# Attention's output in two array steps instead of three, with GELUs on pieces of the pairs

## The chip, the cores and the metric

The kernel runs on one core of a Trainium2 chip. The metric is the device time of one execution in microseconds (us), the median of repeated runs. The core has TensorE (matmul products), VectorE (DVE), ScalarE (ACT), GpSimd (POOL) and SyncE (SP), which issues most of the transfers. The engines work side by side, each through its own list of instructions, and wait for one another at semaphores.

## The reference, cut to what matters

Two layers on a picture of 384 channels and 192 x 192 points. The change concerns the first layer, whose attention runs over channels: 8 heads of 48 channels, 9,216 points after pooling.

```python
x = x + L0(gn(x), ...)                         # gn: group norm, 32 groups
x = x + L1(gn(x), ...)                         # signs, shifted by channel, times signs of weights

def L0(x, ...):                                # cut
    qkv = einsum('bchw,oc->bohw', x, w_qkv) + b_qkv
    qkv = qkv.reshape(b, 3*c, 96, 2, 96, 2).max(axis=(3, 5))
    qkv = conv_3x3_depthwise(qkv, w_dw) + b_dw
    q, k, v = split(qkv, 3)                    # each (8 heads, 48, 9216)
    q, k = q / norm(q), k / norm(k)
    attn = einsum('bhcn,bhdn->bhcd', q, k) * temperature
    out = sum(topk_softmax(attn, n) @ v * a    # four sizes n of top-k
              for n, a in ...)
    out = gelu(out, approximate=False)
    out = repeat(repeat(out, 2, axis=2), 2, axis=3)
    return einsum('bchw,oc->bohw', out, w_proj) + b_proj
```

The four softmaxes are one 48 x 48 matrix per head in the end, and "attention's output" is that matrix times v, per head, followed by the GELU.

## The kernel before

The picture is cut into 24 units of 8 rows. A first pass takes the group norm's sums, a second makes q and k and their products, a third makes v. In the third pass each unit has three steps, one for each group of 128 channels of v. One step is:

```python
def qkv_unit(pqkv, xt, u, m, pl, parts, before=None):
    for r0, nr, c0, ncol in BLOCKS:                       # three blocks of 512 points
        ps = pqkv.tile([P, 512], F32, name="qkv")         # 3 PSUM buffers
        for t in range(CT):
            nc.tensor.matmul(ps, wq[:, t, m*P:(m+1)*P], x4[:, t, ...], ...)       # L351
        nc.vector.tensor_reduce(pl[...], ps..., AX.XY, ALU.max)                   # L358, pooling
    ...
    nc.scalar.activation(new, new, AF.Identity, bias=bq[:, m:m+1])                # L367, the bias
    for acc, r0, n in parts:                              # one chunk, or two at a chunk's edge
        for k in range(9):                                # the 3 x 3 taps
            if k == 0:
                nc.scalar.activation(acc2, src, AF.Identity, bias=..., scale=...) # L374, first tap
            else:
                nc.vector.scalar_tensor_tensor(acc2, src, wdw[...], acc2, ...)    # L376
    if u < NU - 1:
        nc.scalar.copy(pl[:, 0:2, :], pl[:, PR:PR+2, :])                          # L378, the halo
```

v comes to lie in `chunk`, four units to a chunk. Heads go in pairs of 96 channels (`PAIR`), of which there are four (`NP`). Pair p has partitions 32p to 32p+31 (`Q` = 32) of all three groups t: in group 0 the first 32 channels of its first head, in group 1 the first 32 of its second head, and in group 2 the last 16 of both. `aT` holds the matrices, laid out to match, with zeros between the two heads. Whenever a block of 512 points (there are `NAB` = 18) is complete, its output is computed, and written over v:

```python
def attention(g):
    c, b = divmod(g, CPX // ABLK)
    cols = slice(b * ABLK, (b + 1) * ABLK)
    pss = [po.tile([P, ABLK], F32, name="ops") for _ in range(NP)]    # 4 PSUM banks in all
    for t in range(CT):
        for p in range(NP):
            rows = slice(p * Q, (p + 1) * Q)
            nc.tensor.matmul(                                          # L625
                pss[p][:PAIR],
                aT[rows, t, p * PAIR : (p + 1) * PAIR],
                chunk[c][rows, t, cols],
                start=(t == 0), stop=(t == CT - 1),
            )
    for p, ps in enumerate(pss):
        for t in [p] if p < CT else range(CT):
            src, to = (slice(0, PAIR),) * 2 if p < CT else (slice(t * Q, (t + 1) * Q), slice(PAIR, P))
            nc.scalar.activation(chunk[c][to, t, cols], ps[src], AF.Gelu,
                                 accum_out=osum[to, t, g : g + 1])     # L635

for u in range(NU):
    ...
    for m in range(CT):
        qkv_unit(pqkv, xt, u, 2 * CT + m, pool[m], parts)
        ...                                        # softmaxes in pieces, until steps == ()
        elif steps == () and done < NAB - HOLD and (done + 1) * ABLK <= first * WP:
            attention(done)
            done += 1
```

The last two blocks (`HOLD` = 2) come in the tail, where the order is set by hand. Elsewhere a scheduler sets the order of each engine's instructions when the program is built; it keeps the waits, but not the order of the text. After the tail comes the last stage: projection, signs, and the second layer's products.

Of the kernel before, what the change touches and what calls it, by code (L numbers as in the profile page):

```python
# [15 lines left out]
AF = mybir.ActivationFunctionType  # L16
# [4 lines left out]
P = 128  # L21
C = 384
CT = C // P
# [4 lines left out]
HD = C // HEADS  # L28
# [14 lines left out]
HALF = P // 2  # L43
# [8 lines left out]
ABLK = 512  # L52
NAB = NPX // ABLK
# [23 lines left out]
PAIR = 2 * HD  # L77
NP = C // PAIR
Q = P // NP
HOLD = 2  # L80
# [67 lines left out]
def conv_preact_kernel(ctx: ExitStack, tc: tile.TileContext, a: dict, out: bass.AP):  # L148
    nc = tc.nc
# [27 lines left out]
    def unit(u, pool=big, parts=1, pieces=1):  # L177
        xt = pool.tile([P, CT, UPX], F32, name="xt", tag="big")
        n = CT // parts
        for t in range(0, CT, n):  # L180

            for j in range(0, UPX, UPX // pieces if t == CT - 1 else UPX):
                px = slice(j, j + UPX // pieces if t == CT - 1 else UPX)
                nc.sync.dma_start(xt[:, t : t + n, px], xv[u][:, t : t + n, px])  # L184
        return xt
# [15 lines left out]
    def group_sums(ps, s):  # L201

        for t in range(CT):
            nc.tensor.matmul(ps, ind[:, t, :], s[:, t], start=(t == 0), stop=(t == CT - 1))
# [8 lines left out]
    def right(name, bufs=1, stack=att):  # L213
        return stack.enter_context(tc.tile_pool(name=name, bufs=bufs, side="right"))
# [4 lines left out]
    osum = ap.tile([P, CT, NAB], F32, name="osum")  # L219
    aT = right("aT").tile([P, CT, C], F32, name="aT")  # L220
# [35 lines left out]
    with tc.tile_pool(name="p1", bufs=1, side="right") as p1, tc.tile_pool(name="p1ps", bufs=2, space=PSUM) as psp:  # L256
# [17 lines left out]
        for i in range(NU):  # L274
# [8 lines left out]
            for t in range(CT):  # L283
                if t == (u + 1) % SHARE:
                    at = NB + i // SHARE
# [8 lines left out]
                b, k = divmod(seen[t], BATCH)  # L294
                seen[t] += 1
                for j in range(UPX // 512):
                    at = (k * (UPX // 512) + j) * 6
# [5 lines left out]
        with tc.manual_schedule():  # L303
# [5 lines left out]
            ps = psp.tile([NG, 2], F32, name="gsps")  # L309
# [13 lines left out]
            ps = [psp.tile([P, 1, 2], F32, name=f"spread{t}", bufs=1) for t in range(CT)]  # L323
# [15 lines left out]
    def rows(u):  # L339

        return (1 if u else 2), (PR if u < NU - 1 else PR + 1)
# [41 lines left out]
    with pairs, tc.tile_pool(name="p2t", bufs=2, side="right") as tp:  # L383
# [59 lines left out]
        for u in range(NU):  # L443
# [6 lines left out]
            n = hi - lo + 1  # L450
# [11 lines left out]
    def gathered():  # L462

        products(NU - 1)
        for t in range(CT):
            at = D0[t] - B0[t] * B
            nc.vector.tensor_copy(gsb[:, t, : DN[t]], gram[t][:, at : at + DN[t]])
        last_products.close()
# [104 lines left out]
    def opened(name, bufs, **kw):  # L573
        return end.enter_context(tc.tile_pool(name=name, bufs=bufs, reuse_waits="tile", **kw))
# [25 lines left out]
    chunk = []  # L600
    with ExitStack() as vs:
        wp = vs.enter_context(tc.tile_pool(name="p4w", bufs=1, side="right", reuse_waits="tile"))
        scratch = vs.enter_context(ExitStack())
        p3 = right("p3", stack=scratch)
        vs.enter_context(products_of_x)

        pool = first_pooled
        for t in pool:
            nc.gpsimd.memset(t[:, 0:2, :], 0.0)  # L609
        done, steps = 0, None  # L610

        def weights(name):
            wl = wp.tile([P, CT, C], F32, name="wl")
            tc.keep_in_program_order(nc.scalar.dma_start(wl, a[name].rearrange("(t p) o -> p t o", p=P)))
            return wl

        def attention(g):

            c, b = divmod(g, CPX // ABLK)
            cols = slice(b * ABLK, (b + 1) * ABLK)  # L620
            pss = [po.tile([P, ABLK], F32, name="ops") for _ in range(NP)]
            for t in range(CT):
                for p in range(NP):
                    rows = slice(p * Q, (p + 1) * Q)
                    nc.tensor.matmul(  # L625
                        pss[p][:PAIR],
                        aT[rows, t, p * PAIR : (p + 1) * PAIR],
                        chunk[c][rows, t, cols],
                        start=(t == 0),
                        stop=(t == CT - 1),  # L630
                    )
            for p, ps in enumerate(pss):
                for t in [p] if p < CT else range(CT):
                    src, to = (slice(0, PAIR),) * 2 if p < CT else (slice(t * Q, (t + 1) * Q), slice(PAIR, P))
                    nc.scalar.activation(chunk[c][to, t, cols], ps[src], AF.Gelu, accum_out=osum[to, t, g : g + 1])  # L635

        for u in range(NU):
            xt = kept.pop(NU + u) if NU + u in kept else unit(u)
            if u == NU - 1:
                for i, f in enumerate(FIRST):  # L640
                    kept[f] = unit(f, big if i else early)
            if u % UC == 0:
                chunk.append(big.tile([P, CT, CPX], F32, name="chunk", tag="big"))
            lo, hi = rows(u)
            first = PR * u - 2 + lo
            last = first + hi - lo
            for m in range(CT):
                parts = []
                for c in range(first // CR, last // CR + 1):
                    r0, r1 = max(first, c * CR), min(last, c * CR + CR - 1)  # L650
                    parts.append(
                        (chunk[c][:, m, (r0 - c * CR) * WP : (r1 + 1 - c * CR) * WP], r0 - first, r1 + 1 - r0)
                    )
                qkv_unit(pqkv, xt, u, 2 * CT + m, pool[m], parts)
                if m == 0 and u == UC:

                    wl = weights("w_projG").rearrange("p t (g c) -> p t g c", c=GRP)
                    tc.keep_in_program_order(nc.vector.tensor_reduce(wg1, wl, AX.X, ALU.add))
                if m == 0 and u == 1:
                    tc.keep_in_program_order(  # L660
                        nc.scalar.dma_start(wpr, a["w_projT"].rearrange("(t p) o -> p t o", p=P))
                    )
                if m == 0 and u == UC + 1:
                    tc.keep_in_program_order(nc.scalar.activation(wb, weights("weightT"), AF.Sign, saturate=False))
                if u == 0 and m == CT - 1:
                    gathered()
                    po = vs.enter_context(tc.tile_pool(name="p4o", bufs=NP, space=PSUM))
                    psp = vs.enter_context(tc.tile_pool(name="p3ps", bufs=1, space=PSUM))
                    bg = psp.tile([P, P], F32, name="p3ps")[:NG, :1]
                    group_sums(bg, bpr.unsqueeze(2))  # L670
                    nc.vector.tensor_scalar_mul(bg1, bg, -1.0 / GRP)
                if u >= TOPK and steps is None:
                    steps = softmaxes(p3, psp)
                if steps:
                    if next(steps, 1):
                        steps = ()
                        scratch.close()
                        early = opened("p5x0", 1)
                elif steps == () and done < NAB - HOLD and (done + 1) * ABLK <= first * WP:
                    attention(done)  # L680
                    done += 1
        kept[FIRST[1] - 1] = unit(FIRST[1] - 1)
        with tc.manual_schedule():

            assert done == NAB - HOLD
            for g in range(done, NAB - 1):
                attention(g)
            for m in range(CT):
                projected(pqkv.tile([P, 512], F32, name="qkv")[:, :PPX], FIRST[0], m)
            attention(NAB - 1)  # L690

            projected(pqkv.tile([P, 512], F32, name="qkv")[:, :PPX], FIRST[1], 0)
            nc.vector.tensor_reduce(om, osum, AX.X, ALU.add)
            ys = [pqkv.tile([P, 512], F32, name="qkv")[:, :PPX] for m in range(1, CT)]
            projection(ys[0], FIRST[1], 1)
            projection(ys[1], FIRST[1], 2, range(1))
            ps = psp.tile([P, P], F32, name="p3ps")[:NG, :1]
            for t in range(CT):
                nc.tensor.matmul(ps, wg1[:, t], om[:, t : t + 1], start=(t == 0), stop=(t == CT - 1))
            nc.vector.tensor_scalar(gm, ps, -1.0 / (GRP * NPX), bg1, ALU.mult, ALU.add)  # L700
            projection(ys[1], FIRST[1], 2, range(1, 2))
            ps = psp.tile([P, P], F32, name="p3ps")[:, :CT].unsqueeze(2)
            spread(ps, gm)
            projection(ys[1], FIRST[1], 2, range(2, CT))
            added(ys[0], FIRST[1], 1, 0)
            nc.vector.tensor_add(nmean1, nmean0, ps[:, :, 0])
            added(ys[0], FIRST[1], 1, 1)
            for r in range(2):
                added(ys[1], FIRST[1], 2, r)
# [203 lines left out]
```

## Time and profile before

| | before |
|---|---|
| median of 3 runs | 2239.83 us (2238.95 to 2241.53) |
| span of the profiled execution | 2237.0 us |
| TensorE busy | 2085.8 us, 93% |
| VectorE busy | 1902.5 us, 85% |
| ScalarE busy | 819.6 us, 37% |
| GpSimd busy | 210.8 us, 9% |
| granted TensorE clock | 1.0 |
| products of attention's output (L625) | 432 records, 52.0 us busy |
| their GELUs (L635) | 108, of 587 ns each |

Each fp32 matmul of the text is two records in the profile, a pair of passes. A line of groups reads: source line, engine, operation, what is written <- what is read, shape, count, then busy time, mean duration in ns, and the idle time of the engine before these instructions with what ended it. A line of a timeline reads: start in us, duration in us, engine, source line, operation, tensors, shape, count, and in brackets the idle time before it and what ended that. A line of windows gives the stretch, its length, and per engine the busy time and the number of instructions.

### The profile page before, as it was taken

Reading aid. Unit: us, or ns where it says so; the run is one execution under the profiler, and the core shown is the slowest. Engines: PE = TensorE matmul, PEld = TensorE weight load, DVE = VectorE, ACT = ScalarE, POOL = GpSimd, SP = SyncE. Lnnn points to the kernel's source line nnn. Section 1 sums busy time; section 2 is a strip of 40 time slices with the busy share of each in tenths; the row PEclk is TensorE's granted clock in tenths of the full one; section 3 lists DMA queues with packets and bytes.
Section 4 is the critical chain, followed back from the end, with each engine's and each line's share of the span. In section 5 each row is a group of like instructions: output and inputs, shape, how many; then the busy total and the mean of one; then the engine's idle time right before and its main releaser. Section 6 shows DMA issues by size and latency. Waiting matters only on the chain.

```text
span 2237.0 us, 19501 instructions
## 1 busy us (share of the span) xinstructions
PE 2085.8 (93%) x6135; PEld 989.3 (44%) x6135; DVE 1902.5 (85%) x3267; ACT 819.6 (37%) x1419; POOL 210.8 (9%) x329
## 2 busy tenths in 40 slices
PE   0049999999999999999999999999999999999998
PEld 0024444444444444444444444443444444455555
DVE  5668888888888888888888898987787878899998
ACT  4542222222222222222222221225333232398876
POOL 1000000000000000000000000000000000077765
PEclk9999999999999999999999999999999999999999
DMA  9962222222222222222222312105221212379997
GB/s 398 418 274 64 64 68 70 75 95 70 69 64 68 70 74 95 70 69 64 68 70 72 98 30 105 53 11 211 85 85 43 87 67 101 127 277 407 424 425 328
DMA packets 209719, 302.66 MB, mean 135 GB/s; under 512 B 162224, under 2 KB 165072, under 8 KB 209616
## 3 DMA queue, kind: packets, MB, share of 16 engines
q1 hardware_dynamic: 199296, 248.18, 31.8%
q10 hardware_dynamic: 10320, 53.25, 5.8%
q8 instruction: 48, 0.79, 0.1%
q14 instruction: 55, 0.45, 0.1%
HBM read 216.04 MB, written 56.62 MB: 122 GB/s over the span
## 4 chain that ended last, share of the span: by engine, by line
PE 81%; DVE 10%; DMA 5%; ACT 1%; SPq 1%; issue 0%; DVEq 0%; ACTq 0%
PE qkv L351 64%; PE l1ps L792 6%; PE yps L580 6%; DVE chunk L376 5%; DMA xt<-in_x_dram 5%; PE gram L433 3%; DVE pooled L358 2%; PE ops L625 2%; DVE dw L376 1%; SPq L184 1%; DVE xt L592 1%; ACT chunk L374 0%; PE qkv L270 0%; ACT pooled L367 0%; SPq L422 0%
## 5 line engine op out<-in xcount | busy, mean ns | idle before, releaser
L351 PE MATMUL qkv<-xt,wq 128*128 128x512 f32 x3888 | 1679.2, 593 | 0.0
L351 PEld LDWEIGHTS qkv<-xt,wq 128*128 128x128 f32 x3888 | 735.1, 190 | 918.1 <-issue 821.9
L376 DVE SCALAR_TENSOR_TENSOR dw<-pooled,small,dw 128x384 f32<-128x384 f32 (+2 forms) x1152 | 708.7, 615 | 118.8 <-ACT dw L374 93.7
L358 DVE TENSOR_REDUCE pooled<-qkv 128x128 f32<-128x512 f32 x648 | 442.5, 684 | 67.1 <-PE qkv L351 66.8
L376 DVE SCALAR_TENSOR_TENSOR chunk<-pooled,small,chunk 128x384 f32<-128x384 f32 (+3 forms) x696 | 369.5, 545 | 70.9 <-ACT chunk L374 53.7
L378 ACT COPY pooled<-pooled 128x196 f32<-128x196 f32 x207 | 73.6, 356 | 761.5 <-DVE dw L376 542.8
L367 ACT ACTIVATE pooled<-pooled,small 128x384 f32<-128x384 f32 x216 | 133.0, 616 | 402.8 <-DVE pooled L358 389.4
L773 ACT ACTIVATE signs<-xt,nmean 64x1536 fp8e4<-64x1536 f32 x144 | 226.5, 1573 | 41.7 <-PE yps L580 26.0
L792 PE MATMUL l1ps<-signs,wb 128*128 128x384 fp8e4 x864 | 152.2, 326 | 0.0
L580 PE MATMUL yps<-chunk,wpr 128*128 128x384 f32 x396 | 138.2, 487 | 2.7 <-DVE xt L592 2.7
L270 PE MATMUL qkv<-wq,late 128*32 128x384 f32 x18 | 9.0, 665 | 140.3 <-ACT late L292 140.3
L801 DVE SCALAR_TENSOR_TENSOR xt<-l1ps,small,xt 128x768 f32<-128x768 f32 x144 | 138.3, 1007 | 0.0
L592 DVE SCALAR_TENSOR_TENSOR xt<-yps,small,xt 128x768 f32<-128x768 f32 x132 | 128.1, 1012 | 10.8 <-PE yps L580 4.4
L298 DVE BATCH_NORM_STATS2 room<-xt 128x6 f32<-128x512 f32 x144 | 88.1, 678 | 51.0 <-DMA xt<-in_x_dram 50.9
L609 POOL MEMSET pooled<- 128x196 f32 x3 | 0.8, 263 | 1300.6 <-DVE dw L376 1300.6
L456 ACT ACTIVATE sq<-dw 128x384 bf16<-128x384 f32 (+2 forms) x144 | 75.3, 523 | 112.4 <-DVE dw L376 112.4
L792 PEld LDWEIGHTS <-wb 128*128 128x128 fp8e4 x864 | 83.7, 97 | 72.3 <-issue 14.2
L374 ACT ACTIVATE dw<-pooled,small 128x384 f32<-128x384 f32 (+2 forms) x144 | 100.4, 697 | 2.2
L287 ACT ACTIVATE room<-xt 128x1536 bf16<-128x1536 f32 x48 | 71.2, 1483 | 66.4 <-DMA xt<-in_x_dram 65.7
L580 PEld LDWEIGHTS yps<-chunk,wpr 128*128 128x128 f32 x396 | 73.2, 190 | 44.3 <-issue 3.6
L404 DVE STREAM_TRANSPOSE blocks<-dw 128x384 f32<-128x384 f32 (+1 forms) x144 | 82.0, 569 | 3.4
L751 POOL COPY rest<-signs 9x384 int32<-9x384 int32 (+1 forms) x144 | 72.4, 503 | 64.5 <-ACT signs L773 59.0
(115 smaller groups left out, 622.1 us busy)
## 6 DMA issues: line engine op xcount, KB each, us to landing
xt<-in_x_dram SPq DMA_DIRECT2D x81, 2304.0 KB, 13.4
out_dram<-xt ACTq DMA_DIRECT2D x17, 2304.0 KB, 15.6
room<-blocks SPq DMA_DIRECT2D x736, 36.0 KB, 2.0
xt<-in_x_dram SPq DMA_DIRECT2D x26, 768.0 KB, 9.0
out_dram<-xt ACTq DMA_DIRECT2D x12, 768.0 KB, 8.7
out_dram<-xt SPq DMA_DIRECT2D x8, 768.0 KB, 3.4
wq<-in_w_qkvT_dram ACTq DMA_DIRECT2D x1, 1728.0 KB, 15.1
room<-blocks SPq DMA_DIRECT2D x32, 48.0 KB, 2.0
```

What stands on the lines that cost most here:

```text
L298: nc.vector.bn_stats(stats[b][:, t, at : at + 6], xt[:, t, j * 512 : (j + 1) * 512])
L351: nc.tensor.matmul(ps, wq[:, t, m * P : (m + 1) * P], x4[:, t, r0 : r0 + nr, c0 : c0 + ncol], start=(t == 0), stop=(t == CT - 1),)
L358: nc.vector.tensor_reduce(pl[:, 2 + r0 // 2 : 2 + (r0 + nr) // 2, 1 + c0 // 2 : 1 + (c0 + ncol) // 2], ps.rearrange("p (i a j b) -> p i j ...
L367: nc.scalar.activation(new, new, AF.Identity, bias=bq[:, m : m + 1])
L374: nc.scalar.activation(acc2, src, AF.Identity, bias=bdw[:, m : m + 1], scale=wdw[:, m, 0:1])
L376: nc.vector.scalar_tensor_tensor(acc2, src, wdw[:, m, k : k + 1], acc2, ALU.mult, ALU.add)
L404: nc.vector.transpose(to[:, :full], acc[:, : full * P].rearrange("p (k j c) -> p k j c", j=NBP, c=B))
L580: nc.tensor.matmul(ps, wpr[:, t, m * P : (m + 1) * P], o[:, t, :], start=(t == 0), stop=(t == CT - 1),)
L592: nc.vector.scalar_tensor_tensor(x5[:, m, r], yb, bpr[:, m : m + 1], x5[:, m, r], ALU.add, ALU.add)
L773: nc.scalar.activation(rows_of(sg, p, SAT[t] - HSHIFT[t][h]), xt[p, t, :].rearrange("p (r w) -> p r w", w=W), AF.Sign, bias=nmean1[p, t : ...
L792: nc.tensor.matmul(ps[:, j, : 2 * W], wb[:, t, m * P : (m + 1) * P], rows_of(sg, slice(0, P), SAT[t])[:, r0 + 2 * j : r0 + 2 * j + 2], sta ...
L801: nc.vector.scalar_tensor_tensor(blk, ps[:, :, : 2 * W], bl1[:, m : m + 1], blk, ALU.add, ALU.add)
```

## The change

The output of a pair is 96 channels wide, and 32 rows of the array by 96 columns were used by each product. The change uses products of 32 rows and 64 columns. The first half of a pair's columns (channels 0 to 63 of the pair, PSUM partitions 0 to 63) takes group 0 and then group 2, the other half (channels 32 to 95, PSUM partitions 64 to 127) takes group 1 and then group 2. So eight products can be in the array at once, and two steps do what took three. Of the first half channels 0 to 47 are whole, the first head, and of the other channels 48 to 95, the second head; what lies between in each half is incomplete and is not kept.

The output of a pair is now in two places[...], so that a GELU reads and writes pieces: for the first three pairs 32 rows, of which 16 are then written over, 48 and 32; for the fourth pair four pieces of 16 or 32 rows. That is 13 GELUs for a block instead of six. To spread them, `attention` has become a generator: one step of the loop issues the products and the GELUs of the first two pairs, the next step those of the other two. While a block waits for its second part, no new one is begun. The two blocks of the tail keep the old form.

```diff
-            for t in range(CT):
-                for p in range(NP):
-                    rows = slice(p * Q, (p + 1) * Q)
-                    nc.tensor.matmul(
-                        pss[p][:PAIR],
-                        aT[rows, t, p * PAIR : (p + 1) * PAIR],
-                        chunk[c][rows, t, cols],
-                        start=(t == 0),
-                        stop=(t == CT - 1),
-                    )
+            split = g < NAB - HOLD
+            sides = ((0, 0), (PAIR - HALF, HALF)) if split else ((0, 0),)
+            n = HALF if split else PAIR
+            for i in range(2 if split else CT):
+                for h, (o, at) in enumerate(sides):
+                    t = (h, CT - 1)[i] if split else i
+                    for p in range(NP):
+                        rows = slice(p * Q, (p + 1) * Q)
+                        nc.tensor.matmul(
+                            pss[p][at : at + n],
+                            aT[rows, t, p * PAIR + o : p * PAIR + o + n],
+                            chunk[c][rows, t, cols],
+                            start=(i == 0),
+                            stop=(t == CT - 1),
+                        )
             for p, ps in enumerate(pss):
-                for t in [p] if p < CT else range(CT):
-                    src, to = (slice(0, PAIR),) * 2 if p < CT else (slice(t * Q, (t + 1) * Q), slice(PAIR, P))
-                    nc.scalar.activation(chunk[c][to, t, cols], ps[src], AF.Gelu, accum_out=osum[to, t, g : g + 1])
+                if p == NP // 2:
+                    yield
+                if split:
+                    moves = ((HALF, Q, Q), (0, 0, HD), (HALF + Q, 2 * Q, Q))
+                else:
+                    moves = ((0, 0, PAIR),)
+                for at, o, n in moves:
+                    for j in (0,) if p < CT else range(0, n, Q):
+                        if p < CT:
+                            t, to, k = p, o, n
+                        else:
+                            t, to, k = (o + j) // Q, PAIR, min(Q, n - j)
+                        nc.scalar.activation(
+                            chunk[c][to : to + k, t, cols],
+                            ps[at + j : at + j + k],
+                            AF.Gelu,
+                            accum_out=osum[to : to + k, t, g : g + 1],
+                        )
... (cut)
-                elif steps == () and done < NAB - HOLD and (done + 1) * ABLK <= first * WP:
-                    attention(done)
-                    done += 1
+                elif steps == ():
+                    if block:
+                        list(block)
+                        block = None
+                    elif done < NAB - HOLD and (done + 1) * ABLK <= first * WP:
+                        block = attention(done)
+                        next(block)
+                        done += 1
... (cut: the tail calls list(attention(g)))
```

More of the change, by code (lines that the diff above doesn't have):

```diff
@@ L609, in conv_preact_kernel @@
             nc.gpsimd.memset(t[:, 0:2, :], 0.0)
-        done, steps = 0, None
+        done, steps, block = 0, None, None
         def weights(name):
@@ L678, in conv_preact_kernel @@
                         early = opened("p5x0", 1)
-                elif steps == () and done < NAB - HOLD and (done + 1) * ABLK <= first * WP:
-                    attention(done)
-                    done += 1
+                elif steps == ():
[6 more added lines that the diff above has]
+                        done += 1
         kept[FIRST[1] - 1] = unit(FIRST[1] - 1)
         with tc.manual_schedule():
-            assert done == NAB - HOLD
+            assert done == NAB - HOLD and not block
             for g in range(done, NAB - 1):
-                attention(g)
+                list(attention(g))
             for m in range(CT):
                 projected(pqkv.tile([P, 512], F32, name="qkv")[:, :PPX], FIRST[0], m)
-            attention(NAB - 1)
+            list(attention(NAB - 1))
             projected(pqkv.tile([P, 512], F32, name="qkv")[:, :PPX], FIRST[1], 0)
```

## The prediction

> **What bounds the kernel now.** I read the page first (TensorE busy 93% of the span), then the chain of waits, then the windows of the only stage that the change touches, and last the timelines of one attention block there. The groups by form give the block's two halves, its products and its GELUs:
>
> ```profile
> L351 PE MATMUL qkv<-xt,wq 128*128 128x512 f32 x3888 | 1679.2, 593 | 0.0
> ...
> L625 PE MATMUL ops<-chunk,aT 32*96 32x512 f32 x432 | 52.0, 601 | 0.2 <-ACT chunk L635 0.2
> ...
> L635 ACT ACTIVATE chunk<-ops 32x512 f32<-32x512 f32 x54 | 31.7, 587 | 0.8
> L635 ACT ACTIVATE chunk<-ops 96x512 f32<-96x512 f32 x54 | 31.4, 587 | 5.1 <-PE ops L625 4.7
> ```
>
> See that a GELU of 32 rows costs what one of 96 rows costs, 587 ns: on ScalarE the count of instructions decides, not the rows. The stage runs from the first attention product to the products of the tail:
>
> ```profile
> core 0: us, PE busy (x) PEld busy (x) DVE busy (x) ACT busy (x) POOL busy (x), PEclk, DMA share, GB/s
> 1511.70:1938.80 427.10, 426.92 (x1267) 181.97 (x1266) 337.86 (x631) 150.77 (x349) 0.00 (x0) 1.00 0.25 94
> ```
>
> TensorE is never idle in these 427.1 us, at the full clock; VectorE has 89 us idle. So TensorE bounds the stage, and on this view alone less work on TensorE is time won. The timelines of one block show how near the other loop is. TensorE:
>
> ```profile
> 1667.95 2.83 PE L625 MATMUL ops<-chunk,aT 32*96 32x512 f32 x24
> 1670.71 23.44 PE L351 MATMUL qkv<-xt,wq 128*128 128x512 f32 x54
> 1694.08 2.83 PE L625 MATMUL ops<-chunk,aT 32*96 32x512 f32 x24
> ```
>
> A block holds TensorE from 1667.95 to 1670.71, 2.76 us; three channel groups of qkv (a "step" from here: one of the three groups of one unit) take 23.37 us, 7.79 each; the period is 26.13. ScalarE in the same period:
>
> ```profile
> 1673.49 0.36 ACT L378 COPY pooled<-pooled 128x196 f32<-128x196 f32 x1 [3.36 <-DVE chunk L376]
> 1673.88 0.60 ACT L635 ACTIVATE chunk<-ops 96x512 f32<-96x512 f32 x1
> ...
> 1674.46 0.58 ACT L635 ACTIVATE chunk<-ops 96x512 f32<-96x512 f32 x1
> ...
> 1675.74 0.58 ACT L635 ACTIVATE chunk<-ops 32x512 f32<-32x512 f32 x1
> ...
> 1676.54 0.59 ACT L635 ACTIVATE chunk<-ops 32x512 f32<-32x512 f32 x1
> ...
> 1677.73 0.18 ACT L635 ACTIVATION_READ_ACCUMULATOR chunk<-ops 32x1 f32 x1
> 1679.47 0.62 ACT L367 ACTIVATE pooled<-pooled,small 128x384 f32<-128x384 f32 x1 [1.55 <-DVE pooled L358]
> ```
>
> The six GELUs go from 1673.88 to 1677.91, 4.03 us, between the copy of the halo of one step and the bias of the next. That bias then waits only 1.55 us more, for TensorE's last product. VectorE:
>
> ```profile
> 1670.17 5.20 DVE L376 SCALAR_TENSOR_TENSOR chunk<-pooled,small,chunk 128x384 f32<-128x384 f32 x8 [1.42 <-ACT chunk L374]
> ...
> 1680.86 0.62 DVE L376 SCALAR_TENSOR_TENSOR chunk<-pooled,small,chunk 128x384 f32<-128x384 f32 x1 [1.42 <-ACT chunk L374]
> ...
> 1689.02 0.62 DVE L376 SCALAR_TENSOR_TENSOR chunk<-pooled,small,chunk 128x384 f32<-128x384 f32 x1 [1.42 <-ACT chunk L374]
> ...
> 1696.53 0.62 DVE L376 SCALAR_TENSOR_TENSOR chunk<-pooled,small,chunk 128x384 f32<-128x384 f32 x1 [0.90 <-ACT chunk L374]
> ```
>
> Each step's taps wait for ScalarE's first tap, which stands behind the bias, which stands behind the GELUs. So there is a second loop, VectorE to ScalarE and back, with about 1.5 us of slack per block.
>
> **What the Trainium skill says.** "TensorE: Matmul & The Clock Gate", section "Part 3: Packing small matmuls", says that products in different row and column tiles of the array run at the same time, about 4 ns apart, and gives 10.6 times for 16 tiles. The trace agrees for four row tiles: four products start within 20 ns, and the groups of four follow at 0.43 us. No run yet shows column tiles. The same page, "Architectural detail", says that ScalarE and VectorE take their instructions strictly in order; the trace agrees (in the block above the bias comes only after all six GELUs, each first tap after its bias). "ScalarE: Activation LUTs", section "What ACT_TABLE_LOAD costs", says that activations back to back overlap by about 93 ns. The trace agrees only in part: the GELUs of 96 rows start 0.57 to 0.58 us apart, but those of 32 rows, each at other partitions than the one before, 0.69 to 0.80.
>
> **The change part by part.** Products: a block has two passes of each of three steps at 0.43 us, 6 x 0.43 = 2.58, and 0.18 us of first weights. Two steps leave 4 x 0.43 + 0.18 = 1.90. That is 0.86 us less per block, and 16 of the 18 blocks are changed (the last two keep the old form): 13.8 us of TensorE's path, if eight tiles run together.
>
> GELUs: a pair's output now lies in two column halves, so a pair takes three GELUs instead of one, and the fourth pair four instead of three: 3 x 3 + 4 = 13 for 6. Nearly all of them change their partitions from one to the next, so I take the spacing of the 32-row ones: (0.71 + 0.80 + 0.69) / 3 = 0.73. Ten such, two overlapped at 0.57 and a last one of 0.68: 10 x 0.73 + 2 x 0.57 + 0.68 = 9.1; with a wait or two of a GELU on an earlier one whose rows it overwrites, 9.2 us. Before it was 4.03.
>
> Order: "two parts" should put half of the GELUs into one step and half into the next. In ScalarE's instruction order of the built program they are not apart: all 13 stand together between one halo copy and the next bias, 16 times. The spacing of the blocks changes too. In steps, before: five intervals of 1, then 3, 3, 6, 3, 3, 6, 3, 3, 6, 3, 5. After: seven of 2, then 3, 3, 3, 6, 3, 3, 6, 3, 5. Both sum to 49 steps.
>
> The loop after the change, from the start of the eight taps that precede the GELUs, with the durations of the timelines: to the halo copy 3.32, copy 0.39, GELUs 9.2, bias and first tap 1.39, taps and reductions of that step 6.77, next bias and first tap 1.39. That closes an interval of 2 steps: 22.5 us, where TensorE needs 2 x 7.79 + 1.90 = 17.5. An interval of 3 steps adds 6.12 + 1.39: 30.0, where TensorE needs 25.3 and the old kernel took 26.13. The reductions inside don't wait for TensorE then, which is ahead by its three PSUM buffers and stalls when they are full. So the loop of VectorE and ScalarE becomes the bound, and TensorE's 13.8 us are worth nothing.
>
> The sum: 7 x 22.5 = 157; six intervals of 3 steps, 6 x 30.0 = 180; two of 6 steps, each 30.0 and three steps without GELUs at about 7.6 (the reductions of the old kernel's long interval come at that pace), 2 x 52.8 = 106; the last of 5 steps, 30.0 + 2 x 7.7 = 45. Together 488 us for the stage that took 427: 61 more. About four of the GELU groups follow steps at a chunk's edge, where the halo copy comes some 1.9 us after the taps' start and not 3.3, with one more short tap: about 4 less. So 57 us more: 2240 + 57 = 2297 us. What comes before and after the stage is unchanged.
>
> **The rivals.** (1) TensorE stays the bound: all of the gain, -14 us, 2226. For it: TensorE is 100% busy, ScalarE only 35% (150.77 of 427), and seven more short instructions per block fit easily by the sum. Against it: the slack in front of the bias is 1.55 us, the GELUs grow by 5.2. (2) The loop binds, but the GELUs all overlap as the 96-row ones do: 12 x 0.57 + 0.68 = 7.5 us, 1.7 less per block and 16 x 1.7 = 27 less: 2270. For it: several of them wait for a semaphore, as the 96-row ones do. Against it: the first 32-row GELU also waits for one, and started 0.71 after its forerunner. (3) Every GELU at the slowest spacing, 0.80: 10.3 us, 2314. (4) Eight tiles don't run together: a block has four steps, 8 x 0.43 + 0.18 = 3.6 us on TensorE. It alone would make 2253; behind the loop of 22.5 against 2 x 7.79 + 3.6 = 19.2 it stays hidden, so it hardly moves my number.
>
> **Range and chances.** The loop is in program order, with measured parts; the open term is the length of 13 GELUs, 7.5 to 10.3, times 16, which is -27 to +18. Some more lies in how far the steps without GELUs catch up (I gave them nothing: in the 6-step intervals VectorE's pace is near TensorE's). So 2268 to 2318. Over 2% slower begins at 2284.6, inside the range: 0.69. Within 2%: 0.27, for rival 2 and for more catching up than I see. Faster by over 2% has no source: 0.04, for something that I misread altogether.
>
> **What would show it.** Right: in the stage TensorE falls from 100% to near 85% busy, and its idle time is ended by VectorE's reductions; 13 GELUs in one run of about 9 us; the bias behind them starts at once, without the 1.55 us of wait for TensorE; two-step periods of about 22.5 us and three-step ones of 30; the products of a block over 1.9 us. Wrong: biases that still wait for TensorE after the GELUs, or periods of 25.3; or GELUs interleaved with the steps' other work. If the products take 3.6 us, only the step on tiles fails.

## The result, and the profile after

| | before | after |
|---|---|---|
| median | 2239.88 us (2238.95 to 2241.53) | 2312.51 us (2312.03 to 2313.01) |
| span of the profiled execution | 2237.0 us | 2311.2 us |
| stage of the blocks | 427.1 us | 497.2 us |
| what comes after that stage | 298.2 us | 302.4 us |
| TensorE busy in the stage | 426.9 us | 440.1 us |

The ratio is 1.0323, with a 95% interval of 1.0306 to 1.0341: 3.2% slower. 70.1 us of the 74.2 by which the span grew lie in the one stage that the change touches.

First the page of the kernel after, its busy times and the chain of work that ended last:

```profile
PE 2101.2 (91%) x6263; PEld 988.1 (43%) x6263; DVE 1900.2 (82%) x3267; ACT 913.0 (40%) x1643; POOL 210.7 (9%) x329
...
PE 62%; DVE 20%; ACT 10%; DMA 5%; SPq 1%; issue 1%; DVEq 0%; ACTq 0%
PE qkv L351 47%; DVE chunk L376 13%; ACT chunk L656 7%; PE l1ps L823 6%; PE yps L580 5%; DMA xt<-in_x_dram 5%; DVE pooled L358 5%; PE gram L433 3%; ACT chunk L374 1%; ACT pooled L367 1%; DVE dw L376 1%; SPq L184 1%; DVE xt L592 1%; PE qkv L270 0%; SPq L422 0%
```

Before, that chain was:

```profile
PE 81%; DVE 10%; DMA 5%; ACT 1%; SPq 1%; issue 0%; DVEq 0%; ACTq 0%
```

The busy shares hardly tell the story: TensorE still leads with 91%, and ScalarE went from 37% to 40%. The chain does: a fifth of the span has moved from TensorE to VectorE's taps, ScalarE's GELUs (L656, 7%; no GELU was among the lines of the chain before) and VectorE's reductions. Next the groups by form of the kernel after:

```profile
L351 PE MATMUL qkv<-xt,wq 128*128 128x512 f32 x3888 | 1702.5, 598 | 40.0 <-DVE pooled L358 40.0
...
L656 ACT ACTIVATE chunk<-ops 32x512 f32<-32x512 f32 x150 | 88.0, 587 | 2.4
...
L634 PE MATMUL ops<-chunk,aT 32*64 32x512 f32 x512 | 36.1, 648 | 17.1 <-DVE chunk L376 17.1
...
L656 ACT ACTIVATE chunk<-ops 48x512 f32<-48x512 f32 x48 | 28.3, 590 | 1.2
...
L656 ACT ACTIVATE chunk<-ops 16x512 f32<-16x512 f32 x16 | 9.4, 586 | 0.2
```

A GELU of 16 rows takes 586 ns, one of 48 rows 590: thirteen pieces cost thirteen full instructions. The qkv products, which never waited before, now wait 40.0 us for VectorE's reductions. The window of the stage:

```profile
core 0: us, PE busy (x) PEld busy (x) DVE busy (x) ACT busy (x) POOL busy (x), PEclk, DMA share, GB/s
1511.60:2008.80 497.20, 440.08 (x1399) 179.40 (x1398) 334.54 (x629) 244.26 (x573) 0.00 (x0) 0.96 0.21 81
```

TensorE's idle time is 497.20 - 440.08 = 57.1 us, which is the 40.0 and 17.1 of the two groups above: waits for VectorE's reductions and for its last taps. The waits of all engines in this window (total us, times, longest us) show the loop:

```profile
DVE chunk L376 <- ACT chunk L374: 122.3, 37, 8.7
ACT pooled L367 <- DVE pooled L358: 94.5, 33, 6.9
...
PE qkv L351 <- DVE pooled L358: 40.0, 23, 5.5
```

The first of these, before:

```profile
DVE chunk L376 <- ACT chunk L374: 45.1, 37, 1.8
```

Read as a ring: VectorE's taps wait for ScalarE's first tap, that stands behind GELUs and bias, and TensorE waits for the reductions that VectorE does late. One block in the timelines, ScalarE first (the accumulator reads between the GELUs and some GELUs are left out):

```profile
1584.61 0.35 ACT L378 COPY pooled<-pooled 128x196 f32<-128x196 f32 x1 [3.36 <-DVE chunk L376]
1584.99 0.59 ACT L656 ACTIVATE chunk<-ops 32x512 f32<-32x512 f32 x1
...
1586.39 0.59 ACT L656 ACTIVATE chunk<-ops 48x512 f32<-48x512 f32 x1
...
1587.21 0.59 ACT L656 ACTIVATE chunk<-ops 32x512 f32<-32x512 f32 x1
...
1588.03 0.59 ACT L656 ACTIVATE chunk<-ops 48x512 f32<-48x512 f32 x1
...
1595.16 0.61 ACT L367 ACTIVATE pooled<-pooled,small 128x384 f32<-128x384 f32 x1
...
1608.42 0.59 ACT L656 ACTIVATE chunk<-ops 32x512 f32<-32x512 f32 x1
```

Thirteen GELUs in one run, from 1584.99 to the bias at 1595.16: 10.17 us, and the bias has no wait of its own left. The GELUs of the next block, two steps later, begin 23.43 us after these. VectorE in the same block:

```profile
1596.55 0.62 DVE L376 SCALAR_TENSOR_TENSOR chunk<-pooled,small,chunk 128x384 f32<-128x384 f32 x1 [8.27 <-ACT chunk L374]
...
1604.71 5.20 DVE L376 SCALAR_TENSOR_TENSOR chunk<-pooled,small,chunk 128x384 f32<-128x384 f32 x8 [1.42 <-ACT chunk L374]
```

It stands idle for 8.27 us while ScalarE works through the GELUs, where before it waited 1.42 us. And TensorE:

```profile
1598.02 1.97 PE L634 MATMUL ops<-chunk,aT 32*64 32x512 f32 x32
1599.93 7.99 PE L351 MATMUL qkv<-xt,wq 128*128 128x512 f32 x18
1610.57 9.49 PE L351 MATMUL qkv<-xt,wq 128*128 128x512 f32 x18 [2.65 <-DVE pooled L358]
```

The block's products hold it for 1599.93 - 1598.02 = 1.91 us, against 2.76 before. So the products did become faster, and then TensorE waits 2.65 us for a reduction.

### The profile page after: what moved, and what is told of

Same layout as the page of the kernel before. It is cut to its first block, busy times and chain, and to the rows that moved or that the text cites. A ratio compares the mean times of both kernels' runs of the same rounds, so it can differ in the third digit from the quotient of the medians.

```text
span 2311.2 us, 19976 instructions
## 1 busy us (share of the span) xinstructions
PE 2101.2 (91%) x6263; PEld 988.1 (43%) x6263; DVE 1900.2 (82%) x3267; ACT 913.0 (40%) x1643; POOL 210.7 (9%) x329
## 4 chain that ended last, share of the span: by engine, by line
PE 62%; DVE 20%; ACT 10%; DMA 5%; SPq 1%; issue 1%; DVEq 0%; ACTq 0%
PE qkv L351 47%; DVE chunk L376 13%; ACT chunk L656 7%; PE l1ps L823 6%; PE yps L580 5%; DMA xt<-in_x_dram 5%; DVE pooled L358 5%; PE gram L433 3%; ACT chunk L374 1%; ACT pooled L367 1%; DVE dw L376 1%; SPq L184 1%; DVE xt L592 1%; PE qkv L270 0%; SPq L422 0%
## 5 line engine op out<-in xcount | busy, mean ns | idle before, releaser
L351 PE MATMUL qkv<-xt,wq 128*128 128x512 f32 x3888 | 1702.5, 598 | 40.0 <-DVE pooled L358 40.0
L656 ACT ACTIVATE chunk<-ops 32x512 f32<-32x512 f32 (+3 forms) x220 | 129.2, 587 | 6.9 <-PE ops L634 3.2
L823 PEld LDWEIGHTS <-wb 128*128 128x128 fp8e4 x864 | 83.7, 97 | 72.8 <-issue 14.5
```

What stands on the lines that cost most here:

```text
L351: nc.tensor.matmul(ps, wq[:, t, m * P : (m + 1) * P], x4[:, t, r0 : r0 + nr, c0 : c0 + ncol], start=(t == 0), stop=(t == CT - 1),)
L656: nc.scalar.activation(chunk[c][to : to + k, t, cols], ps[at + j : at + j + k], AF.Gelu, accum_out=osum[to : to + k, t, g : g + 1],)
L823: nc.tensor.matmul(ps[:, j, : 2 * W], wb[:, t, m * P : (m + 1) * P], rows_of(sg, slice(0, P), SAT[t])[:, r0 + 2 * j : r0 + 2 * j + 2], sta ...
```

## The experiments

All times are medians; ratios are against the kernel before, run on the same chip. My theory was that of the prediction: 13 GELUs in front of the bias make the loop of VectorE and ScalarE the bound; the products do gain on TensorE, unseen; the two parts don't come apart.

**1. The new products without the pieces.** The change without its 13 GELUs. The six GELUs have the old shapes and read the PSUM partitions 0 to 95 as if the channels still lay there. What is left out is the picking of the right channels out of the two halves; products, calls and the rest are those of the kernel after.

```diff
-                if split:
-                    moves = ((HALF, Q, Q), (0, 0, HD), (HALF + Q, 2 * Q, Q))
-                else:
-                    moves = ((0, 0, PAIR),)
+                moves = ((0, 0, PAIR),)
```

> The products and the spacing of the blocks of the changed kernel, but six GELUs of the old shapes for a block (they read PSUM partitions 0 to 95 as they lie, so that part of the channels is not the right one). Theory (the 13 GELUs hold up the loop of ScalarE and VectorE, and nothing else of the change costs): the two-step loop is 13.3 + 4.0 = 17.3 us, under TensorE's 17.5, so TensorE binds again and the 0.86 us per block come out: 2226 us, 0.994 of before. Rival A (the products with 64 columns, or their waits for the taps, cost the time): it stays near 2310. Rival B (the slower spacing of the blocks, one in two steps, costs): above 2250.

Measured: 2228.32 us (2227.70 to 2229.32), ratio 0.9946 (0.9931 to 0.9961). Its window and its TensorE in one block:

```profile
1511.20:1927.60 416.40, 413.73 (x1395) 174.95 (x1395) 337.43 (x631) 150.77 (x349) 0.00 (x0) 1.00 0.25 97
```

```profile
1581.43 1.97 PE L634 MATMUL ops<-chunk,aT 32*64 32x512 f32 x32
1583.33 15.72 PE L351 MATMUL qkv<-xt,wq 128*128 128x512 f32 x36
1598.98 1.97 PE L634 MATMUL ops<-chunk,aT 32*64 32x512 f32 x32
```

Two steps and a block now take 17.55 us, back to back, and the stage 416.4 us. That is 10.7 us less than before, not 16 x 0.86 = 13.8. Five of the 16 blocks show why:

```profile
1711.14 1.11 PE L634 MATMUL ops<-chunk,aT 32*64 32x512 f32 x16
1712.75 1.12 PE L634 MATMUL ops<-chunk,aT 32*64 32x512 f32 x16 [0.49 <-DVE chunk L376]
1713.80 2.41 PE L351 MATMUL qkv<-xt,wq 128*128 128x512 f32 x5
```

TensorE waits between the first and the second half of the block, until VectorE's last tap of group 2 is written (by VectorE's timeline it ends at 1712.70). The products of group 2 used to come 1.72 us after the block's start, now they come 0.86 us after it, and in these five blocks that is too early: they take 2.66 us. Eleven times 0.86 and five times 0.10 is 10.0, and 10.7 were measured.

**2. The pieces without the new products.** The kernel before, its products of 96 columns and its calls, but each block's output goes through 13 GELUs.

```diff
-                for t in [p] if p < CT else range(CT):
+                split = g < NAB - HOLD
+                for o, n in ((Q, Q), (0, HD), (2 * Q, Q)) if split else ((0, PAIR),):
+                    for j in (0,) if p < CT else range(0, n, Q):
... (the same pieces as after; the source is at the same partitions as the target's rows)
```

> The products of the kernel before, at its spacing of the blocks, but 13 GELUs for a block in the pieces of the change (32, 48 and 32 rows for three pairs, 32, 32, 16 and 32 for the fourth). Theory: one run of 13 takes about 10.1 us, the one-step loop becomes 14 to 15 us where TensorE needs 10.5, the three-step one 30.9: five of about 14.6, seven of 30.9, three of 53.6 and a last one of 46 are 496 us for the stage, so about 2309 us, 1.03 of before. Rival A (the products are what costs): 2240.

Measured: 2310.55 us (2308.98 to 2311.28), ratio 1.0311 (1.0296 to 1.0327), and in the stage:

```profile
1510.90:2003.50 492.60, 457.72 (x1269) 186.31 (x1268) 334.41 (x627) 242.68 (x573) 0.00 (x0) 0.96 0.22 82
```

The pieces alone cost what the whole change costs. With 13 GELUs no gain of the new products is seen: 2310.55 with the old ones, 2312.51 with the new, and the intervals of the two ratios overlap. With six GELUs they are worth 12 us. That is the signature of two bounds of which only one is active. One thing more differs between the two kernels with 13 GELUs, the spacing of the blocks (five intervals of one step here, seven of two there), and it was not tried alone with 13 GELUs.

**3. The calls alone.** The kernel before, with `attention` as the generator of the change and called as in it, at its spacing; the scheduler again puts the six GELUs together.

```diff
             for p, ps in enumerate(pss):
+                if p == NP // 2:
+                    yield
... (cut: the calls in the loop and in the tail, as in the change)
```

> The products and the six GELUs of the kernel before, called as in the change: a generator, blocks at least two steps apart. Theory: the work of TensorE is the same and its loop stays the bound: 2240 us, within 3. Rival B (the spacing of the blocks is what costs): 2260 or more.

Measured: 2241.54 us (2237.03 to 2241.86), ratio 1.0001 (0.9993 to 1.0010). The other spacing of the blocks, with seven intervals of two steps, costs nothing by itself as long as the GELUs are six.

**4. The same 13 GELUs in another order.** Are the GELUs dear by their number or by their order? Here they stay in one run in front of the bias, fixed in the order of the text, but sorted by the partitions that they read and write: first the pieces at 32 of pairs 0, 1 and 2, then those at 0, then those at 64, then the four of pair 3.

```diff
+                kinds = ((HALF, Q, Q), (0, 0, HD), (HALF + Q, 2 * Q, Q))
+                pieces = [(p, p, o, at, n) for at, o, n in kinds for p in range(CT)]
+                pieces += [(CT, (o + j) // Q, PAIR, at + j, min(Q, n - j))
+                           for at, o, n in kinds for j in range(0, n, Q)]
... (one GELU for each piece, kept in program order)
```

> The changed kernel with its 13 GELUs still in one run, but sorted by the partitions that they read and write: the three of PSUM 64 to 95, the three of 0 to 47, the three of 96 to 127, then the four of the last pair. Theory (a GELU overlaps its neighbour only if both use the same partitions; 0.57 us apart then, 0.69 to 0.82 otherwise): the run takes about 8.8 us instead of 10.15, and as the loop binds, 16 x 1.35 = 22 us come out: about 2291. Rival (the spacing goes by the count of rows or by the reading of accumulators): the run stays at 10.1 and the time at 2312.

Measured: 2289.95 us (2289.01 to 2291.05), ratio 1.0223 (1.0207 to 1.0238). ScalarE's timeline, the first four GELUs and the bias behind the last:

```profile
1725.98 0.59 ACT L650 ACTIVATE chunk<-ops 32x512 f32<-32x512 f32 x1
1726.58 0.20 ACT L650 ACTIVATION_READ_ACCUMULATOR chunk<-ops 32x1 f32 x1
1726.69 0.57 ACT L650 ACTIVATE chunk<-ops 32x512 f32<-32x512 f32 x1
1727.17 0.18 ACT L650 ACTIVATION_READ_ACCUMULATOR chunk<-ops 32x1 f32 x1
1727.26 0.57 ACT L650 ACTIVATE chunk<-ops 32x512 f32<-32x512 f32 x1
1727.74 0.19 ACT L650 ACTIVATION_READ_ACCUMULATOR chunk<-ops 32x1 f32 x1
1727.95 0.59 ACT L650 ACTIVATE chunk<-ops 48x512 f32<-48x512 f32 x1
...
1734.80 0.62 ACT L367 ACTIVATE pooled<-pooled,small 128x384 f32<-128x384 f32 x1
```

The run is 8.82 us long where it was 10.17, and the kernel 22.6 us faster than after the change: 16 x 1.35 = 21.6. The time follows the length of the run almost one for one, as it does only for what lies on the path. And the spacing has a pattern: the second GELU, with the partitions of the first, is followed by the next of its kind after 0.57 us; the third, which is followed by one at other partitions, after 0.69.

**5. The two parts really apart.** The change as it is, with its GELUs kept in program order, so that six come behind the halo copy of one step and seven behind that of the next.

```diff
-                        nc.scalar.activation(
+                        pin = tc.keep_in_program_order if split else (lambda ins: ins)
+                        ins = nc.scalar.activation(
...
+                        pin(ins)
```

> The changed kernel with its GELUs kept apart as its text has them: six right behind the halo copy of the block's step, seven behind that of the next. Theory (each part delays the bias behind it by what it lacks of slack): the two-step loop is 3.7 + 4.7 + 1.4 for the first part, 4.2 + 5.5 + 1.4 for the second, 20.9 us, the three-step loop 28.4; with seven, six, two longer ones and the last some 40 us less than the changed kernel: about 2272 us. So two parts behind the halo copies would be slower than before too. Rival (two parts as such are enough): 2235 or less.

Measured: 2297.19 us (2295.91 to 2298.60), ratio 1.0254 (1.0240 to 1.0268). This was a miss by 25 us: it is 15 us better than the change, and far from what was expected. TensorE in a block shows one wait that was overlooked:

```profile
1598.04 2.24 PE L634 MATMUL ops<-chunk,aT 32*64 32x512 f32 x6
1602.12 3.38 PE L634 MATMUL ops<-chunk,aT 32*64 32x512 f32 x26 [1.83 <-ACT chunk L657]
1605.43 15.94 PE L351 MATMUL qkv<-xt,wq 128*128 128x512 f32 x36
```

The block's products hold TensorE from 1598.04 to 1605.43, 7.39 us. The wait between is not for data to multiply but for room: the four PSUM banks are still being read by the GELUs of the block before, whose second part now ends one step later (the last of them starts at 1601.39, ends at 1601.98, and the products go on at 1602.12). The waits of this kernel in the stage:

```profile
DVE pooled L358 <- PE qkv L351: 53.2, 35, 3.3
...
PE ops L634 <- DVE chunk L376: 18.0, 5, 4.6
PE ops L634 <- ACT chunk L657: 14.9, 10, 2.6
```

VectorE waits 53.2 us for TensorE, where it was 28.5 before. So the loop now passes through TensorE too: GELUs, banks, products, qkv products, reductions, bias, GELUs. TensorE's waits for the banks are 14.9 us in all; in five later blocks it waits for the taps of group 2, 18.0 us, as it does in the kernel after (17.1). How much of the 25 us each of these makes was not worked out.

**6. The parts in front of the halo copy.** ScalarE has a wait of 3.4 us before each halo copy, until VectorE is done with the taps. Here each part is put there, between a step's first tap and its halo copy.

```diff
+        if between:
+            between()                       # begins a block, or ends the one begun
         if u < NU - 1:
-            nc.scalar.copy(pl[:, 0:2, :], pl[:, PR : PR + 2, :])
+            halo = nc.scalar.copy(pl[:, 0:2, :], pl[:, PR : PR + 2, :])
+            if between:
+                tc.keep_in_program_order(halo)
... (cut: GELUs kept in program order as in 5; the loop's own calls go)
```

> The changed kernel, with each part of the GELUs pinned between the first tap of a step and its halo copy, one part (6 or 7 GELUs) to a step. There ScalarE has 6.8 us until the next bias is due, and a part takes 4.9 or 5.7. Theory: no bias waits for a GELU any more, TensorE binds, and the change brings what its products save: about 2226 us, 0.994 of before. Rival C (ScalarE's sum of work is what costs, wherever the GELUs stand): above 2260.

Measured: 2233.14 us (2230.78 to 2234.98), ratio 0.9965 (0.9952 to 0.9977). The mechanism holds: with 13 GELUs of the old order the kernel is below the one before. 7 us of the gain are missing. Part of them stands in two blocks of the two-step stretch, as in the one here:

```profile
1637.28 1.08 PE L638 MATMUL ops<-chunk,aT 32*64 32x512 f32 x6
1638.97 1.96 PE L638 MATMUL ops<-chunk,aT 32*64 32x512 f32 x26 [0.61 <-ACT chunk L661]
1640.85 23.48 PE L351 MATMUL qkv<-xt,wq 128*128 128x512 f32 x54
```

It is the wait of experiment 5 again, smaller: this block holds TensorE for 3.57 us instead of 1.90, another one for 3.0. Five more take 2.66, with the wait for the tap of experiment 1. Together these seven blocks take 6.6 us more than 1.90 each.

**7. The same, begun at one fixed step of a unit.** Both waits have to do with when a block begins. Here a block begins only at group 1 of a unit, so at least three steps after the one before, and group 2 of the units that it reads has been done well before.

```diff
-                    elif done < NAB - HOLD and (done + 1) * ABLK <= first * WP:
+                    elif m == 1 and done < NAB - HOLD and (done + 1) * ABLK <= first * WP:
```

> As the run with the parts between the first tap and the halo copy, but every block begins after the second channel group of a unit, so that there are three steps from one to the next: the products of group 2 then come well after that group's last tap, and the PSUM banks are free. Theory (what that run lacked to the full gain were five blocks whose products waited 0.75 us for a tap, and two that waited 1.1 and 1.7 us for a GELU): all 16 blocks take 1.9 us of TensorE, the stage is 16 x 0.86 = 13.8 us shorter than before, about 2226.5 us. Rival: it stays at 2233, and the rest was lost elsewhere.

Measured: 2228.92 us (2226.74 to 2230.11), ratio 0.9949 (0.9937 to 0.9962). Its window, ScalarE in a block, and the group of its products:

```profile
1511.00:1926.40 415.40, 413.20 (x1395) 175.40 (x1394) 339.98 (x632) 246.32 (x573) 0.00 (x0) 1.00 0.26 97
```

```profile
1615.41 0.71 ACT L374 ACTIVATE chunk<-pooled,small 128x384 f32<-128x384 f32 x1
1616.14 0.59 ACT L661 ACTIVATE chunk<-ops 32x512 f32<-32x512 f32 x1
...
1620.27 0.59 ACT L661 ACTIVATE chunk<-ops 32x512 f32<-32x512 f32 x1
...
1621.09 0.36 ACT L380 COPY pooled<-pooled 128x196 f32<-128x196 f32 x1
...
1624.82 0.62 ACT L367 ACTIVATE pooled<-pooled,small 128x384 f32<-128x384 f32 x1 [2.88 <-DVE pooled L358]
```

```profile
L638 PE MATMUL ops<-chunk,aT 32*64 32x512 f32 x512 | 31.6, 600 | 0.0
```

Six GELUs fill the time before the halo copy, and the bias waits again for VectorE's reductions, 2.88 us, so ScalarE has slack. No product of a block waits: 0.0 in the group, and all 16 blocks hold TensorE for 1.90 us. The stage is 11.7 us shorter than before; 2.2 us of TensorE's idle time are left in it, and 13.8 - 2.2 = 11.6. This version computes all that the kernel before computes, and is faster than both: 0.5% below before, 3.6% below after. With all 13 GELUs it is where experiment 1 was with six (2228.32 us).

## Why the prediction was right, and where it was off

2297 us were predicted, 2312.5 came; the direction and the cause hold, and some terms were mis-sized.

- **The bound changes to the loop of VectorE and ScalarE.** Shown. TensorE falls from 100% to 440.1 of 497.2, 89%, and 40.0 of its 57.1 us of waits end with reductions; experiment 2 gets the whole loss without touching the products, and experiment 4 gets 22.6 us back by sorting the run alone. I said near 85%. The predicted TensorE work was the stage's 427 less 14; but the qkv products took longer in the stage (below). That is not what the loop waited for: VectorE's reductions waited 14.5 us for TensorE in the stage, 28.5 before.
- **All 13 GELUs stand together.** Shown in the timeline; the generator spread nothing.
- **Their length, 9.2 us: this term was too small.** I took 0.73 us a piece, the mean of three spacings, of which only one, 0.80, belongs to a GELU that wrote other partitions than its forerunner and whose successor read others than it. In the kernel after most are of this kind, 0.81 to 0.83 us apart, and the run takes 10.17 us. The size was that of rival 3, whose 10.3 us and 2314 stood in the range. By ScalarE three of the seven two-step periods are 23.42 to 23.43 us, not 22.5, and three of the six three-step ones 30.93, not 30.0: 0.93 more in both.
- **The sum over the intervals came out in part by luck.** 0.93 us in all 16 would be 15 us, and 2297 + 15 = 2312 is what was measured; but two other errors partly cancel behind it, the chunk's edges and the 4 us that came after the stage. By ScalarE the seven two-step periods sum to 158.1 us, not 7 x 23.43 = 164.0: three of them, with steps at a chunk's edge, took 20.5 to 21.6 us. So the edges take 5.9 us off these periods alone, where about 4 had been taken off for all. By the starts of the products on TensorE the stage divides into 158.2 us for seven of two steps (157 predicted), 184.0 for six of three (180), 107.1 for two of six (106) and 47.9 for the last (45). Together 497.2, against 488 - 4. TensorE runs ahead by its buffers, so its single intervals scatter (17.6 to 26.2 us for two steps).
- **The products, 13.8 us in all.** 1.90 us a block is right (1.91), and as predicted it is worth nothing behind the loop. But 13.8 was the value for the case that TensorE binds (rival 1), and there it is 10.7 as the change places its blocks: in five of 16 blocks 0.76 of the 0.86 us are lost to the tap of group 2, which I had left out. In the kernel after the same wait is longer, 17.1 us in five blocks, and stands behind the loop.
- **"What comes after the stage is unchanged": off by 4 us.** 302.4 against 298.2.
- **Rivals.** Rival 1 is false for the change; its bound, TensorE, holds as soon as the GELUs are few (experiment 1) or stand elsewhere (experiment 7). Rival 2, 0.57 throughout, is false: only neighbours with the same partitions are so close. Rival 4 is false: eight tiles do run together.

Beyond the prediction, experiment 5 falsified a thought that the diff suggests, that spreading the GELUs would have saved the change. Where a part lands counted twice there: against the bias, and against the banks that the next block's products wait for.

## What to carry to other kernels

When a change makes its busiest engine faster and gives another engine more instructions, find the slack of that other engine in the place in the order where the instructions go, not its idle time in sum: ScalarE was idle for two thirds of the stage, and had 1.55 us where 13 GELUs came to stand. A GELU of 16 rows took as long as one of 96 here, 586 and 587 ns, so count such pieces by number. And ask what a piece of work that is put off keeps occupied: in experiment 5 the second part held the banks that the next block's products waited for. With the same pieces in front of a copy that waits anyway, begun at a fixed step, a loss of 3.2% became a gain of 0.5%.

## What the runs showed of the hardware

- **GELUs from PSUM with an accumulated sum were spaced by partitions.** One takes 586 to 590 ns for 16 to 96 rows, and its accumulator read 0.18 to 0.20 us. In experiments 4 and 5, where the order is that of the text, the spacing inside a run, where no GELU waits for products, is 0.57 us if the GELU begins to write at the same partition as the one before and the next reads from the same one as it, 0.68 to 0.72 if one of the two changes, and 0.81 to 0.84 if both do (in experiment 5, 1587.22 to 1588.05). The accumulator read starts 0.47 to 0.50 or 0.60 to 0.61 us after its GELU, and the next GELU 0.09 to 0.11 or 0.19 to 0.24 after that. The Trainium skill, "ScalarE: Activation LUTs", section "What ACT_TABLE_LOAD costs", gives about 93 ns of overlap for activations back to back. The lines of experiment 4 agree where the partitions stay, from a GELU to its accumulator read (1726.69 + 0.57 = 1727.26, and the read starts at 1727.17); where they change there is none (1725.98 + 0.59 = 1726.57, and the read starts at 1726.58).
- **Eight tiles run together.** In the block at 1598.02 us of the kernel after, eight products of 32 rows and 64 columns start within 46 ns; the next eight follow after 0.48 us, the others after 0.43. "TensorE: Matmul & The Clock Gate", section "Part 3: Packing small matmuls", says about 4 ns from one tile to the next; here it is 6 to 7.
- **The granted clock was lower in the stage where TensorE stalled most.** In the stage it is 0.96 in the kernel after and in experiments 2 and 4, 0.95 in experiment 5, and 1.00 before and in the others, where TensorE is idle for 3.5 us of the stage at most. The qkv products took 618 ns on the mean in the stage of the kernel after (594 before). The part behind the stage took 302.1 to 303.7 us in the kernel after and in experiments 2 and 5, 298.2 before; but 300.0 in experiment 4 and 301.0 in experiment 6, so it does not simply go with the clock of the stage. Which is cause and which effect, and where those 4 us lie, was not tried.
